# A two-layer graph kernel: neighbour lists for groups of 16 nodes instead of 32, sums on 32x32 tiles of TensorE, two blocks of nodes at a time

## The chip, the cores and the metric

One core of a Trainium2 chip runs the whole program. The metric is the device time of one execution in microseconds (us). Engines are named as in the profile: PE (TensorE matmul), PEld (its weight loads), DVE (VectorE), ACT (ScalarE), POOL (GpSimd), SP (SyncE, which here only issues DMAs).

## The reference

Two graph layers on N = 3327 nodes with D = 512 features. adj is sparse: the average row holds a few entries, but nodes with a low index have many (hubs).

```
# layer 0
h   = relu(layernorm(x));            x = x + adj @ (relu(adj @ (h @ W1) + b1) @ W2) + b2
# layer 1, on h = relu(layernorm(x))
sum_a  = adj @ h                                          # also adj @ (h @ W_gcnb)
attn_a = sigmoid([sum_a, h] @ Wa.T + ba);  attn_b = sigmoid([sum_a, h] @ Wb.T + bb)
hw     = h @ W_sa
e      = where(adj != 0, exp(-leaky_relu(hw @ a_left + (hw @ a_right).T)), 0)
x_a    = (e / (e.sum(1) + 1e-5)) @ hw;     x_b = adj @ (h @ W_gcnb) + b_gcnb
x      = x + sigmoid(attn_a * x_a + attn_b * x_b)
```

## The kernel before

N is padded to 3328: 26 blocks of 128 nodes (block 0 holds the hubs). The host hands over adj transposed, so that 128 rows of adjT are 128 source nodes (the contraction) and its columns are targets. All is float32.

**Stage A, first pass over adj (0 to about 232 us).** The columns of adjT are taken in seven chunks from the back, six of 512 and the last of 256. For each chunk 26 tiles of 128 rows are loaded on SP's queue (`load_adj`, a pool of eight buffers) and multiplied into `acc_u` (L568). DVE reduces each tile to the largest absolute value per group of 32 columns (`most`, L572). During the first chunk x is loaded and normalized as well and u = h @ W1 is made.
From `most` a generator, `make_lists`, makes the neighbour lists of a chunk while the next chunk is multiplied; one step of the generator is taken per tile. For each group of GW = 32 targets and each half (64 rows) of a block of lists, it holds which source nodes have an entry. It flags non-empty columns, scans them (L443 to L459), counts with two small matmuls (L465, L466) and one shifted matmul (L476), compares the place numbers with each row's offset (`at`, L502, on DVE), picks with small matmuls (`p_list`, L513), and turns the result into row numbers (L519 to L533): `row_h` for the rows of h, `row_a` for the pieces of adj. A list is padded to a fixed number of places: 64 places are one "room". `rooms` gives the rooms of each block, 0 for block 0 (done densely), then 8, 7, 6, 5, 5, six times 4, and 3 for the rest. If a list were longer, a dense fallback at the end of the program would run; with these inputs it does not.
As soon as lists are there, POOL gathers the 32-wide pieces of adj that they name (`gather`, L166, out is `ae`), one gather of 128 rows after another; `gather_behind` puts one behind three of four matmuls. At a chunk's end ACT makes gT (L343) and issues DMAs on its own queue: weights, the hub columns, the rows of g (`g_rows`), and for the ten blocks in OWN the block's own diagonal part (`load_own`), for which then no list entry is needed.

**Stage B, second pass (about 232 to 471 us).** The chunks 0 to 2303 are multiplied densely with g (`acc_g`, L825). For the last two chunks (blocks 18 to 25) the same product is made from the lists: 48 gathers of g rows and `acc_s` (L784), at the tiles named in SUMS. `make_h1` then makes x1 and h of layer 1 (`px` L663, layernorm, `score` L623, `own_logits` L630) and stores the rows of h in DRAM. `own_logits` is left for stage C in the blocks of LATE and OWN. Between tiles the hub block is done densely (`acc_hub`, L709).

**Stage C, attention (first gather of h at 455.6 us, to the end).** Blocks 25 down to 1, one at a time:
- `attend`: POOL gathers the h rows of the block's lists (128 rows of 2080 bytes each, out is `hr` or `rows`), DVE and ACT make the masked exponentials beside the adj pieces in `ae` (L950, L954, L249 to L251, L959). `fetch_ae` puts two gathers of adj (AE_PER) between, as long as there are any.
- `sums` (L981): for each list, adj and exponentials together (64 columns) times the gathered rows. A matmul uses a 64x64 tile of the array, that is, a quarter.
- `copy_out` (ACT, L1054, L1058), `turn` (transposes L995, DVE copy L1010), `weigh` (products `p_b` L1035 and `p_a` L1042), `finish`.
On PE the order is written out: weigh(block i+2), turn(block i+1), sums(block i). `pace` lets the first gather of a block wait for the sums of the block LEAD = 3 (in the last part of the blocks: 4) places earlier, so that POOL doesn't run into buffers in use. `issue_after` (here `queued`) keeps the written order on each engine.

```
columns = gather_adj()                     # a generator: one gather of adj at a time
NR, GR, AE_PER = 12, 24, 2
pairs = cycle(rows[1:3] + own + rows[3:] + rows[:1])   # 16 buffers of two rows per partition
```

Of the kernel before, what the change touches and what calls it, by code (L numbers as in the profile page):

```python
# [9 lines left out]
F32 = mybir.dt.float32  # L10
# [10 lines left out]
GW = 32  # L21
NQ = P // GW
HALF = P // 2
ROW = 520
LEAD = 3, 4
# [13 lines left out]
LATE = 10, 11, 16  # L39

OWN = 1, 6, 7, 8, 12, 13, 14, 15, 17, 18


def list_rooms(n_blocks):

    rooms = [0, 8, 7, 6, 5, 5] + 6 * [4]
    return (rooms + n_blocks * [3])[:n_blocks]
# [3 lines left out]
def kernel(  # L51
# [35 lines left out]
    rooms = list_rooms(NB)  # L87
    extra = [int(i in OWN) for i in range(NB)]
    first = [2 * sum(rooms[:i]) for i in range(NB)]
    NL = 2 * sum(rooms)  # L90


# [21 lines left out]
    for _ in range(WAKE):  # L114
# [21 lines left out]
    ae = [  # L136
        kept([P, 2 * (r + extra[i]), 2 * GW], f"ae{i}") if r else None for i, r in enumerate(rooms)
    ]

    def segments(i):  # L140

        r = rooms[i] + extra[i]
        n = -(-r // SEG)
        cuts = [-(-r * k // n) for k in range(n + 1)]
        return list(zip(cuts, cuts[1:]))
    hubp = ctx.enter_context(tc.tile_pool(name="hubp", bufs=6))
# [26 lines left out]
    listed, fetched = set(), [0] * NB  # L173

    def gather_adj():

        order = []
        for n, (c0, w) in enumerate(back):
            order += range(c0 // P, (c0 + w) // P)[:: 1 if n < LISTED else -1]
        for i in order:  # L180
            if not i:
                continue
            r = rooms[i]
            for k0, k1 in segments(i):
                for q in range(2):
                    for k in range(max(k0, extra[i]), k1):
                        while (i, q) not in listed:
                            yield None
                        f = first[i] + q * r + k - extra[i]
                        fetched[i] += 1  # L190
                        yield gather(
                            ae[i][:, 2 * k0 + q * (k1 - k0) + k - k0, :GW], adj_groups,
                            row_a[:, f : f + 1], NP * NG - 1,
                        )

    def load_own(i):

        n = segments(i)[0][1]
        for h in range(2):
            rows = slice(i * P + h * HALF, i * P + (h + 1) * HALF)  # L200
            nc.scalar.dma_start(
                ae[i][h * HALF : (h + 1) * HALF, 0 : n + 1 : n, :GW],
                adjT[rows, rows].rearrange("j (q i) -> j q i", i=GW),
            )
# [54 lines left out]
    with (  # L259
        tc.tile_pool(name="l0", bufs=1) as l0,  # L260
        tc.tile_pool(name="l0w", bufs=2) as l0w,
        tc.tile_pool(name="adjp", bufs=8) as adjp,
    ):

        def load_adj(j, c, name, n=1):

            c0, w = c
            t = adjp.tile([P, CW], F32, tag="adj", name=f"{name}_{c0}_{j}")
# [100 lines left out]
        lower = kept0([P, 1], "lower", F32)  # L369
        place_row = kept0([P, max(rooms) * HALF], "place_row", F16)  # L370
# [3 lines left out]
        def make_constants():  # L374
# [4 lines left out]
            for h in range(2):  # L379
                nc.vector.memset(apart[h * HALF : (h + 1) * HALF, 2 * h : 2 * h + 2], 0.0)  # L380
# [6 lines left out]
            for t, op, base in ((before, ALU.is_gt, 0), (shift, ALU.is_equal, -1)):  # L387
# [7 lines left out]
            nc.vector.memset(lower, 1.0)  # L395
            nc.gpsimd.affine_select(
                lower, lower, pattern=[[0, 1]], compare_op=ALU.is_ge, fill=0.0, base=-HALF,
                channel_multiplier=1,
            )
            first_iota = nc.gpsimd.iota(  # L400
                place_row, pattern=[[1, max(rooms) * HALF]], base=0, channel_multiplier=0,
# [9 lines left out]
            for r in sorted(set(rooms[1:])):  # L411
                i0, n = rooms.index(r), rooms.count(r)
                cols = slice(first[i0], first[i0] + n * 2 * r)
                nc.gpsimd.memset(limit[:, NQ * i0 : NQ * (i0 + n)], float(r * HALF))
# [907 lines left out]
```

## Time and profile before

| | |
|---|---|
| runs | 829.47, 836.75, 842.9 us; median 836.75 |
| the profiled execution | 834.5 us, span from first to last instruction 832.8 |
| busy: PE, DVE, POOL, ACT | 735.6, 506.0, 461.1, 194.5 us |
| granted TensorE clock, mean | 0.94 |
| gathers on POOL (L166) | 436: 194 of adj, 194 of h (120 to `hr`, 74 to `rows`), 48 of g |
| sums L981 | 480 + 296 + 80 matmuls |
| DMA | 185.08 MB, 222 GB/s over the span |

The profile comes from one execution and its page gives busy times by engine, the chain of work that ended last (each piece followed back to what released it), and groups of instructions by source line with busy time, mean duration in ns, and the idle time before them with its releaser. A window is a stretch of the span with the busy time of each engine in it. In POOL's timeline each line is one gather with the idle time before it in brackets.

### The profile page before, as it was taken

The numbers are of one execution on the slowest core, as the hardware profiler recorded it, in microseconds if no ns is written. First come the engines' busy times: TensorE is split into PE (matmuls) and PEld (weight loads), VectorE is DVE, ScalarE is ACT, GpSimd is POOL, SyncE is SP. The second block draws the span as 40 slices with busy tenths as digits, with TensorE's granted clock in tenths as the row PEclk, the third lists the DMA queues.
The fourth block names the chain that finished last, engine by engine and source line by source line (L and its number), as shares of the span: only waits on it lengthen the run. The fifth ranks groups of instructions, "written<-read, shape, count | busy, mean of one in ns | idle before, by whom it ended". The sixth has DMA issues, their size and how long they took to land.

```text
span 832.8 us, 11907 instructions
## 1 busy us (share of the span) xinstructions
PE 735.6 (88%) x3595; PEld 404.5 (49%) x3595; DVE 506.0 (61%) x1625; ACT 194.5 (23%) x402; POOL 461.1 (55%) x490
## 2 busy tenths in 40 slices
PE   9999888989899771999899749967999999999995
PEld 7774333444543220444355236633656655665554
DVE  7778868898860611798987225523665557553552
ACT  7770000000000110354544002211212222221121
POOL 2201756766657776534456766674657666767500
PEclk9999989999999875999999969996999999999999
DMA  8788988988878844789994755664667877767510
GB/s 271 245 287 259 326 246 242 293 272 246 232 232 284 262 132 134 240 279 312 327 314 135 241 150 145 199 185 115 195 211 244 255 206 233 240 205 234 178 51 29
DMA packets 104889, 185.08 MB, mean 222 GB/s; under 512 B 18401, under 2 KB 35441, under 8 KB 104818
## 3 DMA queue, kind: packets, MB, share of 16 engines
q1 hardware_dynamic: 66544, 113.43, 41.8%
q0 software_dynamic: 23264, 57.64, 24.3%
q10 hardware_dynamic: 15010, 13.18, 4.9%
q8 instruction: 30, 0.49, 0.2%
q14 instruction: 41, 0.34, 0.1%
HBM read 162.29 MB, written 22.26 MB: 222 GB/s over the span
## 4 chain that ended last, share of the span: by engine, by line
PE 72%; DVE 7%; issue 6%; another core or an unknown queue 6%; DMA 5%; ACT 2%; POOL 1%; SPq 1%; DVEq 0%; ACTq 0%; POOLq 0%
PE acc_u L568 17%; PE acc L981 12%; PE p_b L1035 11%; PE p_a L1042 10%; PE acc_g L825 8%; PE pu L333 3%; PE ptt L995 3%; DMA a<-in_adjT_dram 2%; PE acc_hub L709 2%; PE px L663 2%; PE pt L325 1%; DMA xb<-in_x_dram 1%; PE acc_s L784 1%; DMA hr<-h_rows,row_h 1%
## 5 line engine op out<-in xcount | busy, mean ns | idle before, releaser
L166 POOL DMA_INDIRECT ae<-in_adjT_dram,row_a x194 | 202.6, 1044 | 181.8 <-DVE past L519 54.3
L568 PE MATMUL acc_u<-a,rows 128*128 128x512 f32 (+1 forms) x364 | 161.0, 583 | 0.5 <-DMA a<-in_adjT_dram 0.5
L166 POOL DMA_INDIRECT hr<-h_rows,row_h x120 | 122.7, 1022 | 62.5 <-issue 27.4
L825 PE MATMUL acc_g<-a,g 128*128 128x512 f32 (+1 forms) x260 | 117.1, 584 | 7.2 <-DMA a<-in_adjT_dram 6.8
L572 DVE TENSOR_REDUCE most<-a 128x16 f32<-128x512 f32 (+1 forms) x182 | 112.3, 638 | 11.6 <-issue 6.3
L1035 PE MATMUL p_b<-W_g_sb,tyT 128*128 128x257 f32 x416 | 99.3, 391 | 15.8 <-DVE tyT L1010 15.3
L1035 PEld LDWEIGHTS p_b<-W_g_sb,tyT 128*128 128x128 f32 x416 | 77.8, 192 | 46.5 <-DVE tyT L1010 15.6
L166 POOL DMA_INDIRECT rows<-h_rows,row_h x74 | 75.1, 1015 | 44.3 <-PE acc L981 20.9
L568 PEld LDWEIGHTS acc_u<-a,rows 128*128 128x128 f32 x364 | 67.2, 195 | 58.8 <-issue 56.0
L1042 PE MATMUL p_a<-W_sa_sb,tyT 128*128 128x512 f32 (+2 forms) x216 | 94.2, 577 | 0.2
L1010 DVE COPY tyT<-ptt 128x512 f32<-128x512 f32 x51 | 34.8, 685 | 87.0 <-PE p_a L1042 31.7
L825 PEld LDWEIGHTS acc_g<-a,g 128*128 128x128 f32 x260 | 50.0, 200 | 58.5 <-issue 44.9
L981 PE MATMUL acc<-hr,ae 64*64 64x512 f32 x480 | 68.3, 614 | 4.4 <-issue 4.0
L166 POOL DMA_INDIRECT g_row<-g_rows,row_h x48 | 49.0, 1021 | 20.9 <-issue 13.4
L1042 PEld LDWEIGHTS p_a<-W_sa_sb,tyT 128*128 128x128 f32 x216 | 40.7, 189 | 38.8 <-issue 36.9
L884 ACT ACTIVATE f<-f 128x2 f32<-128x2 f32 x26 | 5.3, 203 | 192.4 <-DVE f L883 97.2
L981 PEld LDWEIGHTS acc<-hr,ae 64*64 64x64 f32 x480 | 27.6, 136 | 33.6 <-issue 33.0
L343 ACT ACTIVATE gT<-acc_u,b_col 128x512 f32<-128x512 f32 (+1 forms) x7 | 4.6, 656 | 163.8 <-DMA a<-in_adjT_dram 90.9
L663 PE MATMUL px<-W_sb,sT 128*128 128x512 f32 x52 | 26.7, 650 | 15.4 <-ACT sT L799 12.0
L666 DVE TENSOR_TENSOR xb<-px,xb 128x512 f32<-128x512 f32 x26 | 17.3, 682 | 36.6 <-PE px L663 28.5
L981 PE MATMUL acc<-rows,ae 64*64 64x512 f32 x296 | 37.1, 593 | 2.5 <-issue 2.3
L623 DVE SCALAR_TENSOR_TENSOR junk<-rows,w_rows 128x512 bf16<-128x512 f32 x52 | 35.6, 684 | 3.2 <-ACT rows L244 1.1
(159 smaller groups left out, 945.2 us busy)
## 6 DMA issues: line engine op xcount, KB each, us to landing
a<-in_adjT_dram SPq DMA_DIRECT2D x286, 256.0 KB
h_rows<-rows SPq DMA_DIRECT2D x26, 260.0 KB
x<-in_x_dram SPq DMA_DIRECT2D x26, 256.0 KB
xb<-in_x_dram SPq DMA_DIRECT2D x26, 256.0 KB
x<-xb ACTq DMA_DIRECT2D x26, 256.0 KB
x1b<-x SPq DMA_DIRECT2D x26, 256.0 KB
out_dram<-va SPq DMA_DIRECT2D x25, 256.0 KB
ae<-in_adjT_dram,row_a POOLq DMA_INDIRECT x194
```

What stands on the lines that cost most here:

```text
L166: return nc.gpsimd.indirect_dma_start(out=dst, out_offset=None, in_=table, in_offset=bass.IndirectOffsetOnAxis(ap=rows, axis=0), bounds_ch ...
L333: nc.tensor.matmul(pu[:, :HID], hT[:, k, :], W1_sb[:, k, :], start=(k == 0), stop=(k == KD - 1))
L568: added = nc.tensor.matmul(acc[:, :w], u[j], a[:, :w], start=(j == 0), stop=(j == NB - 1))
L572: nc.vector.tensor_reduce(most[:, : w // GW, j], a[:, :w].rearrange("p (b i) -> p b i", i=GW), axis=AX.X, op=ALU.max, apply_absolute_value ...
L623: return nc.vector.scalar_tensor_tensor(junk, h, 1.0, w_rows[:, s, :], op0=ALU.mult, op1=ALU.mult, accum_out=into)
L663: last_row[2] = nc.tensor.matmul(px, sT[:, b * P : (b + 1) * P], W2_sb, start=True, stop=True)
L825: added = nc.tensor.matmul(acc[:, :w], g[j], a[:, n % per, :], start=(n == 0), stop=(n == NB - 1))
L981: added = nc.tensor.matmul(taken[i]["acc"][h][q * HALF : (q + 1) * HALF, :], both[half_p, q * n + k, :], taken[i][k0][k][half_p, q, :D], s ...
L995: moved = nc.tensor.transpose(pt[:, k * P : (k + 1) * P], ty[h][:, k * P : (k + 1) * P], ident)
L1010: last = nc.vector.tensor_copy(dst, src)
L1035: nc.tensor.matmul(p_b[n][:, :WH], tyT[:, k, 0, :], W_g_sb[:, k, n * WH : (n + 1) * WH], start=(k == 0), stop=(k == KD - 1),)
L1042: last = nc.tensor.matmul(p_a[:, c0:c1], tyT[:, k, 1, :], W_sa_sb[:, k, c0:c1], start=(k == 0), stop=(k == KD - 1),)
```

## The change

- Lists are made for groups of 16 targets (GW = 16). Blocks are handled in teams: block 1 alone, and twelve pairs (2,3) to (24,25). A pair's 128 partitions are cut into four quarters: two blocks by two halves; a room is then 32 places for each of them. Rooms per team are 5, 7, 5, 5, 4, 4, 4, 4, 3, 3, 3, 3, 3, with four lists (q) each: 53 x 4 = 212 gathers of adj and as many of h. All pairs load their own diagonal parts, by eight DMAs per pair, and their own h rows.
- `sums` works on 32x32 tiles: four quarters (r) by four lists (q), each 512 columns.
- In stage C the order is one team at a time: weigh and turn for the two blocks of the team before (`weigh_all`, with a `turn` between `p_b` and `p_a` of the last), then the team's sums. LEAD is 2 teams; `fetch_ae` takes four gathers per team. Block 0 is copied and turned before the first sums.
- The comparisons `at` are made by ACT as a steep sigmoid (STEEP = 200) instead of by DVE.
- adj is loaded in pieces of two tiles (512 KB), five buffers; `most` is reduced over two tiles at once.
- LATE grows from three to nine blocks; no block's `own_logits` is skipped in stage B on account of OWN. The list sums of stage B use a copy of the adj pieces that ACT places in a 32-wide tile (`diag`), and start at other tiles (SUMS).

```diff
-GW = 32
+GW = 16
-LEAD = 3, 4
+LEAD = 2
-LATE = 10, 11, 16
-OWN = 1, 6, 7, 8, 12, 13, 14, 15, 17, 18
-    rooms = [0, 8, 7, 6, 5, 5] + 6 * [4]
-    return (rooms + n_blocks * [3])[:n_blocks]
+LATE = 8, 10, 11, 12, 13, 14, 15, 16, 17
+def make_teams(n_blocks):
+    teams = [(1,)] + [(i, i + 1) for i in range(2, n_blocks, 2)]
+    rooms = [5, 7, 5, 5, 4, 4, 4, 4] + n_blocks * [3]
+    return teams, rooms[: len(teams)]
...
+    def tiles_of(m):
+        return [
+            (slice(r * tall[m], (r + 1) * tall[m]), teams[m][r // 2], r % 2)
+            for r in range(P // tall[m])
+        ]
...
+    def load_own(m):
+        n = segments(m)[0][1]
+        for part, i, h in tiles_of(m):
+            for s in range(2):
+                nodes = own_rows(i, h, s)
+                nc.scalar.dma_start(
+                    ae[m][part, 2 * s * n : (2 * s + 1) * n + 1 : n, :GW],
+                    adjT[nodes, nodes].rearrange("j (q i) -> j q i", i=GW),
+                )
...
-        tc.tile_pool(name="adjp", bufs=8) as adjp,
+        tc.tile_pool(name="adjp", bufs=5) as adjp,
...
-            t = adjp.tile([P, CW], F32, tag="adj", name=f"{name}_{c0}_{j}")
+            t = adjp.tile([P, 2 * CW], F32, tag="adj", name=f"{name}_{c0}_{j}")
...
-                        nc.vector.tensor_scalar(
-                            at[:, k : k + r, h, :],
-                            place_row[:, : r * HALF].rearrange("p (k m) -> p k m", m=HALF),
-                            offset[:, b : b + 1], None, op0=ALU.is_ge,
-                        )
+                        nc.scalar.activation(
+                            at[:, k : k + r, part],
+                            place_row[:, : r * t].rearrange("p (k m) -> p k m", m=t),
+                            AF.Sigmoid, bias=offset[:, b : b + 1], scale=STEEP,
+                        )
...
-                with queued(scaled[min(j + 3, NB - 1)] if n == 0 else None):
-                    nc.vector.tensor_reduce(
-                        most[:, : w // GW, j], a[:, :w].rearrange("p (b i) -> p b i", i=GW),
+                both = 2 if n else 1
+                if j % both == 0:
+                    tiles = tile_a[:, j % per : j % per + both, :]
...
-        SUMS = {1: (14, 16, 18, 20, 24), 2: (16, 18, 20, 22, 25)}
+        SUMS = {1: (2, 15, 19, 24), 2: (3, 17, 21, 25)}
...
             for k in range(n):
-                for q in range(2):
-                    for h in range(2):
-                        half_p = slice(h * HALF, (h + 1) * HALF)
+                for q in range(4):
+                    for r, (part, i, h) in enumerate(tiles_of(m)):
                         added = nc.tensor.matmul(
-                            taken[i]["acc"][h][q * HALF : (q + 1) * HALF, :],
-                            both[half_p, q * n + k, :], taken[i][k0][k][half_p, q, :D],
+                            taken[m]["acc"][r][q * QW : (q + 1) * QW, :],
+                            both[part, q * n + k, :], taken[m][k0][k][q][part, :D],
...
+        for m in range(M - 1, 0, -1):
+            with queued(*held):
+                for seg in segments(m):
+                    made = attend(m, seg)
...
+            fetch_ae(2 * AE_PER)
+            held, turned = [], []
+            added = weigh_all(added)
+            with queued(added):
+                for seg in segments(m):
+                    added = sums(m, seg)
```

## The prediction

> **What bounds the kernel now.** I read the page first: busy times, then the chain that ended last, then the costliest groups; after that the windows by stage, and at last POOL's own timeline. The page:
>
> ```profile
> PE 735.6 (88%) x3595; PEld 404.5 (49%) x3595; DVE 506.0 (61%) x1625; ACT 194.5 (23%) x402; POOL 461.1 (55%) x490
> PE 72%; DVE 7%; issue 6%; another core or an unknown queue 6%; DMA 5%; ACT 2%; POOL 1%; SPq 1%; DVEq 0%; ACTq 0%; POOLq 0%
> L166 POOL DMA_INDIRECT ae<-in_adjT_dram,row_a x194 | 202.6, 1044 | 181.8 <-DVE past L519 54.3
> L166 POOL DMA_INDIRECT hr<-h_rows,row_h x120 | 122.7, 1022 | 62.5 <-issue 27.4
> L981 PE MATMUL acc<-hr,ae 64*64 64x512 f32 x480 | 68.3, 614 | 4.4 <-issue 4.0
> ```
>
> PE is the bound by share, and the listed sums (L981) are 12% of the chain. POOL looks free at 55%. The windows (stage A: first pass over adj with the lists; B: second pass; C: attention) correct that; the columns are the stretch, its length, then PE, PEld, DVE, ACT and POOL busy, granted clock, DMA share, GB/s:
>
> ```profile
> 0.00:232.00 232.00, 212.82 (x1104) 121.25 (x1104) 189.29 (x532) 51.20 (x113) 113.03 (x153) 0.96 0.85 263
> 320.00:440.00 120.00, 102.52 (x358) 48.84 (x357) 92.61 (x308) 50.63 (x85) 57.50 (x54) 0.93 0.85 279
> 560.00:786.00 226.00, 217.44 (x1210) 126.88 (x1209) 118.63 (x428) 49.52 (x109) 146.84 (x144) 0.96 0.70 212
> 786.00:833.00 47.00, 37.52 (x228) 23.29 (x226) 21.84 (x78) 9.38 (x22) 0.00 (x0) 0.95 0.13 42
> ```
>
> A lives on DMA (0.85), PE and DVE close together; C is PE's, and POOL has nothing after 786. But POOL's busy time leaves out what it does between gathers. Its timeline (start, length, idle before in brackets), and two pieces of the chain in time:
>
> ```profile
> 577.46 0.99 POOL L166 DMA_INDIRECT rows<-h_rows,row_h  x1 [7.54 <-PE acc L981]
> 578.76 1.00 POOL L166 DMA_INDIRECT rows<-h_rows,row_h  x1 [0.31 <-issue]
> 580.07 1.00 POOL L166 DMA_INDIRECT rows<-h_rows,row_h  x1 [0.30 <-issue]
> ...
> 585.28 1.00 POOL L166 DMA_INDIRECT ae<-in_adjT_dram,row_a  x1 [0.30 <-issue]
> 586.58 0.99 POOL L166 DMA_INDIRECT ae<-in_adjT_dram,row_a  x1 [0.31 <-issue]
> ```
> ```profile
> 473.05 16.46 another core or an unknown queue
> ...
> 585.37 3.49 PE acc L981 x30
> 588.86 3.67 PE p_b L1035 x16
> 592.53 3.43 PE p_a L1042 x8
> ```
>
> Back to back a gather takes one step of 1.303 us, whether its rows are of adj or of h. Stage C runs 217 of them (194 of h, 23 of adj) from 455.6 to 785.3: 217 x 1.303 = 283 of 330 us. So POOL has 47 us of idle time in C, nearly all of it the wait for the sums of an earlier block (`pace`, releaser PE L981 above). That is the cover this change uses.
>
> **The change part by part.** The sum is made against the profiled execution: 834.5 us, span 832.8 (1.7 around it). The median of the runs is 836.75, 1.0027 times that.
>
> *Sums on 32x32 tiles.* Before: 856 instructions (480+296+80); a block of 32 takes 3.49 us, 0.109 us each, so 93 us of PE. A full-array 512-column instruction takes 3.43/8 = 0.43 us (p_a), so four tiles side by side lose nothing. After: 12 pairs x 2 x 16 tiles x (48+12 rooms)/12 = 1920, plus 80 for block 1: 2000. Sixteen side by side: 0.43/16 = 0.027 us, 54 us, saves 39. No row shows 16 tiles. The nearest from the other side is the list sums (L784, 64x32, 128 columns): 24 in some 0.82 us, 0.034 each, whatever the width: 68 us, saves 25. Only if tiles of this size did not overlap further would it be 0.109: 218 us, loses 125. I take 68, the row nearest in shape.
>
> [...]
>
> What PE needs in C is then 26 x (10.8 - 2.63 of sums) = 212 us for turns and products (10.8 us is the step from p_b to p_b of a three-room block) plus 68: 280 us, against 305 before.
>
> *Gathers.* Rooms: 53 x 4 = 212 lists of adj and 212 of h, against 194 each: +36, 47 us of POOL. The built order of POOL's queue says where: before the first h gather 169 adj gathers stand (171 before), so C gets 43 of them (23 before). C on POOL: (212+43) x 1.303 = 332.3 us, +49.5. By team: a three-room pair asks 16 gathers, 20.8 us, of POOL and 2 x 8.17 + 32x4x0.034 = 20.7 of PE: even. Four rooms: 26 to 21.8; five: 31 to 23. So POOL sets C, and the 25 us that PE saves turn into waits of PE for gathered rows. Halving the row of an adj gather (128 to 64 bytes) doesn't help: the step is the same for 2080-byte rows.
>
> How much of the 47 idle us stays? LEAD is now two pairs, four blocks, about as far ahead as before, and PE is faster, so pacing waits shrink: 5 us (start-up only) to 47 (as now). I take 18, because PE is as slow as POOL in the five three-room pairs, and because of the stall of 16.46 us above: PE, ACT and DVE stood during a run of 24 gathers without a gap (455.6 to 486.7) and went on some 3 us after POOL paused. Pieces of the same name stand in B at 265 (9.13), 308 (8.78) and 318 (13.65). The cause isn't in the trace; but C will now be one long run of gathers. The tail after the last gather was 47.5 us, with PE two blocks behind; the least is the last sums to the end, 810.1 to 832.8, plus one attend, 28. I take 38.
>
> *Lists in A.* p_list goes from 388 to 808 matmuls; a group of 12 takes 0.29 to 0.36 us between acc_u steps, so 420 x 0.027 = 11 us more of PE, which the DMA share of 0.85 hides in part; bare it is 11. DVE loses about 100 comparisons (0.22 us from start to start, 22 us); it gains twice the width in flag, scan, after and step (0.46+1.01+0.58+0.58 = 2.6 a chunk, 16 in all); the reduction over two tiles saves the fixed part of one per pair (L572: 676 ns at 512 columns, 408 at 256, so 140 ns fixed; 13 a chunk, 11 us in six). About 17 us of 189 less. ACT gains 200 sigmoids (the 192-wide activation took 0.369, the 128-wide 0.305: 61 to 74 us), one table load of 1.28, and 76 more own-part DMA issues at some 0.65 us (49 us), plus 16 for g_own. ACT is busy 51 of 232 us, so it fits; but within a chunk eight issues per pair stand ahead of the sigmoids, so the lists come late: in the built order most p_list groups stand after tiles 12 to 26 of the 26, where before they stood after tiles 8 to 14. Behind a p_list that waits on ACT stand acc_u, then gT, and the next chunk. Cost: from -10 (DVE relieved, DMA free) to 6 chunks x 6 us = +36. I take +5.
>
> [...]
>
> *adj in pieces of two tiles.* 143 loads for 286, ten tiles in flight for eight. SP's queue issues half as many; the bytes and the DMA share stay. acc_g's wait for adj is 6.8 us in all, so at most 7 gained, and at the start of a chunk a piece of 512 KB lands later than one of 256. Taken at 0, between -7 and +4.
>
> *B.* Nine blocks are LATE and no OWN block is skipped, so 17 instead of 13 own_logits run in B, at 1.7 us of DVE: +7 in a stretch where DVE is busy 93 of 120. List sums get 16 copies on ACT (0.37 each, 6 us, ACT 51 of 120: at nothing; 6 bare). I take +5 for B (0 to 13). The nine late ones (15 us of DVE, 5 before) lie under the first gathers of C, 12 us to the first rows' landing; 0 taken, 10 at most.
>
> *Sum.* First h gather 455.6 + 5 (A) + 5 (B) + 332.3 (gathers) + 18 (pauses) + 38 (tail) = 853.9; + 1.7 = 855.6; x 1.0027 = **858 us**.
>
> **The rivals.**
> *Faster: the stalls go.* Against 858: B's three pieces (9.13+8.78+13.65 = 31.6 us) vanish, and pauses fall from 18 to 4: 858 - 46 = 812. For it: list sums and their gathers start earlier in B and are spread, DVE does less in A, and pieces of adj are larger. Against: 217 gathers precede C, as many as before less two. It decides from 38 us on, the distance from 858 to 820.
> *No change: the idle time takes it all.* +49.5 of gathers into 47 us of idle, A and B at nothing, tail as before: 834.5 + 2.5 = 837, x 1.0027 = 839. For it: POOL's waits in C are nearly all `pace`. Against: a queue without slack passes on every hiccup.
> *Late lists.* PE waits 6 us for ACT's sigmoids in each of six chunks: 858 + 31 = 889.
> *Sixteen tiles are no faster than four:* 839 + 125 = 964. Against: 64x32 tiles already go at 0.034.
>
> **How the numbers follow.** Forecast 0.40; faster 0.32; no change 0.21; late lists 0.05; no overlap 0.02. The three runs before spread by 13 us, 1.6%, so 2% is about what a measurement can tell. Slower: 0.40+0.05+0.02 = 0.47. The range goes from 803 (the faster rival with DMA's -10 in A) to 890 (late lists); the forecast alone, by pauses 5 to 47 with tails 28 to 47 not both at their ends, is 832 to 885.
>
> **What would show it.** Right: in C, POOL's gathers at 1.303 us with idle under 25 us in all, PE idle before L-sums on hr or rows by a DMA releaser; a pair's 32-tile sums at 0.03 to 0.04 us each; gT times later by a few us each chunk. Wrong: POOL paused by PE as often as now (then PE, not POOL, bounds C); sums at 0.1 us; B 30 us shorter or a first h gather well ahead of 455.

## The result and the profile after

The changed kernel takes **1024.52 us** (median of 4 runs, 1013.93 to 1029.38) beside 839.83 us of the kernel before on the same chip (4 runs, 829.47 to 843.69). The ratio is 1.2255, with a 95% interval of 1.204 to 1.2471: 22 to 23% slower. This ratio, like all that follow, is that of the means of the runs within 1.5% of each kernel's fastest, the others (the profiled one here, by a hair) counting as slow. The profiled execution took 1029.38 us, with a span of 1027.6. The forecast was 858, in a range of 803 to 890. The sign was right, the size was not.

The page of the changed kernel, the lines that answer to those shown of before (L178 is `gather`, L1054 is `sums`):

```profile
PE 835.4 (81%) x5221; PEld 417.7 (41%) x5221; DVE 494.6 (48%) x1463; ACT 263.6 (26%) x625; POOL 499.8 (49%) x510
PE 48%; DVE 12%; another core or an unknown queue 12%; DMA 11%; issue 10%; ACT 4%; POOL 2%; ACTq 1%; SPq 0%; POOLq 0%; DVEq 0%
L178 POOL DMA_INDIRECT hr<-h_rows,row_h x140 | 141.2, 1008 | 126.1 <-PE acc L1054 73.9
L178 POOL DMA_INDIRECT rows<-h_rows,row_h x72 | 73.4, 1019 | 72.5 <-PE acc L1054 50.0
L1054 PE MATMUL acc<-hr,ae 32*32 32x512 f32 (+1 forms) x1040 | 108.5, 810 | 9.5 <-issue 8.8
L1054 PE MATMUL acc<-h_own,ae 32*32 32x512 f32 x384 | 40.9, 882 | 85.5 <-DVE tyT L1083 66.3
```

Before, the gathers of h into `rows` stood as

```profile
L166 POOL DMA_INDIRECT rows<-h_rows,row_h x74 | 75.1, 1015 | 44.3 <-PE acc L981 20.9
```

Two readings decide. POOL waits for PE's sums before its gathers of h, more than before (73.9 and 50.0 us, lines 3 and 4), which the forecast named as a sign of being wrong; and PE now waits 66.3 us for DVE before its sums (last line of the page's), for a copy `tyT` of 0.7 us. PE's share of the chain fell from 72% to 48%, and "another core or an unknown queue" doubled to 12%. The windows by stage (length; PE, PEld, DVE, ACT, POOL busy; granted clock, DMA share, GB/s): the first pass A from 65, stage B, C from the first to the last gather of h, and the tail:

```profile
65.00:278.00 213.00, 174.24 (x1101) 73.82 (x1100) 138.36 (x238) 65.99 (x208) 107.42 (x100) 0.89 0.73 216
278.00:506.90 228.90, 186.85 (x759) 85.92 (x760) 136.42 (x463) 78.36 (x157) 125.93 (x117) 0.89 0.71 223
506.90:967.40 460.50, 361.64 (x2658) 179.10 (x2658) 148.84 (x524) 61.23 (x129) 258.07 (x255) 0.83 0.59 164
967.40:1027.60 60.20, 49.24 (x316) 29.80 (x315) 21.15 (x69) 11.56 (x26) 0.00 (x0) 0.94 0.14 45
```

Against the same points of before (last gT 231.6, first gather of h 455.6, last one's end 785.3, end 832.8) A (last gT at 277.9) lost 46.3 us, B 5.0, C 130.8 and the tail 12.7: together 194.8, the difference of the spans. In C the clock is 0.83 and the DMA share 0.59, PE is busy 361.64 and POOL 258.07 of 460.50 us: nothing is full. The chain shows what happens in one team (start, length, what):

```profile
695.69 10.84 another core or an unknown queue
...
707.58 4.62 another core or an unknown queue
...
712.97 8.70 PE acc L1054 x152
```

And three engines in the same stretch, first POOL (in brackets the idle time before, and its releaser), then DVE, then PE:

```profile
683.63 1.00 POOL L178 DMA_INDIRECT hr<-h_rows,row_h  x1 [10.63 <-PE acc L1054]
...
708.75 1.00 POOL L178 DMA_INDIRECT ae<-in_adjT_dram,row_a  x1 [0.31 <-issue]
722.04 1.00 POOL L178 DMA_INDIRECT rows<-h_rows,row_h  x1 [12.29 <-PE acc L1054]
```
```profile
694.94 0.75 DVE L966 SCALAR_TENSOR_TENSOR vb<-vb,r,va 128x512 f32<-128x512 f32 x1 [0.81 <-issue]
706.55 0.43 DVE L961 TENSOR_TENSOR vb<-p_b,bg_row 128x257 f32<-128x257 f32 x1 [10.87 <-remote]
```
```profile
691.42 3.63 PE L1108 MATMUL p_b<-W_g_sb,tyT 128*128 128x257 f32 x16
...
699.50 1.05 PE L1054 MATMUL acc<-h_own,ae 32*32 32x512 f32 x4
712.97 1.75 PE L1054 MATMUL acc<-h_own,ae 32*32 32x512 f32 x14 [12.42 <-DVE tyT L1083]
```

POOL runs 20 gathers without a break, 683.63 to 709.75. PE's records of the `p_b` that DVE waits for end at 695.05; DVE goes on only at 706.55, and for the next piece at 712.22, 2.5 us after POOL has stopped. PE waits for that copy and goes on with its sums at 712.97, after a first four. POOL's next run waits (`pace`) for these sums and starts at 722.04. So POOL and PE take turns: run of gathers, then sums, then the next run. It looks like the 16.46 us stall of before, now in most teams. I call it the hold-up: while POOL's gathers run on without a break, PE's completions (or its work) come some 8 to 17 us late.

The trace of before holds a second one in C, which the prediction does not name. POOL ran 24 gathers from 538.89 to 569.92; the block's `p_b` came 30.9 us after the one before instead of 10.8 to 11.7, and DVE stood:

```profile
572.87 0.43 DVE L891 TENSOR_TENSOR vb<-p_b,bg_row 128x257 f32<-128x257 f32 x1 [13.76 <-remote]
```

The three pieces in B (265, 308, 318 us) lie in or just behind runs of 24 (240.10 to 271.72) and 20 (302.42 to 328.14) as well.

### The profile page after: what moved, and what is told of

Its sections match the earlier page's. It is cut to its first block, busy times and chain, and to the rows that moved or that the text cites. A ratio compares the mean times of both kernels' runs of the same rounds, so it can differ in the third digit from the quotient of the medians.

```text
span 1027.6 us, 15177 instructions
## 1 busy us (share of the span) xinstructions
PE 835.4 (81%) x5221; PEld 417.7 (41%) x5221; DVE 494.6 (48%) x1463; ACT 263.6 (26%) x625; POOL 499.8 (49%) x510
## 2 busy tenths in 40 slices
DMA packets 113127, 192.96 MB, mean 188 GB/s; under 512 B 23197, under 2 KB 40721, under 8 KB 113042
## 4 chain that ended last, share of the span: by engine, by line
PE 48%; DVE 12%; another core or an unknown queue 12%; DMA 11%; issue 10%; ACT 4%; POOL 2%; ACTq 1%; SPq 0%; POOLq 0%; DVEq 0%
PE acc L1054 16%; PE acc_u L607 6%; PE acc_g L895 6%; PE p_b L1108 5%; PE p_a L1116 4%; DMA a<-in_adjT_dram 4%; PE pu L348 2%; DMA xb<-in_x_dram 2%; DVE most L614 2%; DMA ae<-in_adjT_dram 2%; PE acc_hub L767 2%; POOL hr L178 1%; DVE tyT L1083 1%; ACT at L531 1%
## 5 line engine op out<-in xcount | busy, mean ns | idle before, releaser
L178 POOL DMA_INDIRECT ae<-in_adjT_dram,row_a x212 | 227.1, 1071 | 221.1 <-PE acc_u L607 90.6
L178 POOL DMA_INDIRECT hr<-h_rows,row_h x140 | 141.2, 1008 | 126.1 <-PE acc L1054 73.9
L607 PE MATMUL acc_u<-a,rows 128*128 128x512 f32 (+1 forms) x364 | 177.2, 610 | 6.3 <-issue 4.5
L614 DVE TENSOR_REDUCE most<-a 128x64 f32<-128x1024 f32 (+1 forms) x104 | 104.1, 1012 | 54.2 <-DMA a<-in_adjT_dram 42.8
L1054 PE MATMUL acc<-hr,ae 32*32 32x512 f32 (+1 forms) x1040 | 108.5, 810 | 9.5 <-issue 8.8
L1054 PE MATMUL acc<-h_own,ae 32*32 32x512 f32 x384 | 40.9, 882 | 85.5 <-DVE tyT L1083 66.3
L178 POOL DMA_INDIRECT rows<-h_rows,row_h x72 | 73.4, 1019 | 72.5 <-PE acc L1054 50.0
L531 ACT ACTIVATE at<-place_row,offset 128x96 bf16<-128x96 f16 (+4 forms) x200 | 61.1, 393 | 108.7 <-DMA a<-in_adjT_dram 57.2
L1054 PE MATMUL acc<-rows,ae 32*32 32x512 f32 x576 | 64.8, 808 | 3.7 <-issue 3.3
L178 POOL DMA_INDIRECT g_row<-g_rows,row_h x48 | 49.8, 1037 | 31.8 <-ACT at L531 14.8
L1054 PEld LDWEIGHTS acc<-hr,ae 32*32 32x32 f32 (+1 forms) x1040 | 33.2, 121 | 69.9 <-issue 66.3
L961 DVE TENSOR_TENSOR vb<-p_b,bg_row 128x257 f32<-128x257 f32 x26 | 11.1, 426 | 84.9 <-remote 62.1
L1054 PEld LDWEIGHTS acc<-h_own,ae 32*32 32x32 f32 x384 | 6.9, 122 | 102.4 <-DVE tyT L1083 80.2
```

The source lines that it names most:

```text
L178: return nc.gpsimd.indirect_dma_start(out=dst, out_offset=None, in_=table, in_offset=bass.IndirectOffsetOnAxis(ap=rows, axis=0), bounds_ch ...
L531: nc.scalar.activation(at[:, k : k + r, part], place_row[:, : r * t].rearrange("p (k m) -> p k m", m=t), AF.Sigmoid, bias=offset[:, b : b ...
L607: added = nc.tensor.matmul(acc[:, :w], u[j], a[:, :w], start=(j == 0), stop=(j == NB - 1))
L614: nc.vector.tensor_reduce(most[:, : w // GW, j : j + both], tiles.rearrange("p k (b i) -> p b k i", i=GW), axis=AX.X, op=ALU.max, apply_ab ...
L961: read_b = nc.vector.tensor_tensor(vb[:, :WH], p_b[0][:, :WH], bg_row[:, :WH], ALU.add)
L1054: added = nc.tensor.matmul(taken[m]["acc"][r][q * QW : (q + 1) * QW, :], both[part, q * n + k, :], taken[m][k0][k][q][part, :D], start=(k0 ...
```

## The experiments

The first theory: a long unbroken run of gathers holds PE up, whatever the bytes, and `pace` then makes POOL wait in turn. Its rivals: the bytes do it; POOL's rate alone does it; the 32x32 sums themselves are dear; and for A, the lists, the pieces of adj, or ACT.

The kernels ran in several groups. In a group all ran on one chip, beside the kernel before. There were two kinds of chip: on one kind the kernel before takes 829 to 842 us (medians), on the other 734 to 739. On the second kind the hold-up didn't appear. "Kind of chip" is a reading: each chip was used once, and the groups on the first kind all ran before those on the second, so a state that changed with time isn't told apart from the chip. Each number stands beside its own before.

### Runs of 8 to 12 in place of 16 to 20 (e1_spread)

```diff
+                        if k0 + k == extra[m] + 2 and not q and len(combined) >= LEAD:
+                            pace(gathered[0], marks[-1])
...
+            marks.append(last)        # the last p_b of the team's second block
```


> The changed kernel, with one more pace in each team: the gathers of the third room and what follows wait for the p_b of the second block of the team before, so that POOL's 16 to 20 gathers come in runs of about 8 and 8 to 12 with a pause between. Theory A (in a run of more than some nine gathers without a pause the completions of PE reach the other engines late, until the run ends; then POOL's run and PE's sums follow each other instead of overlapping): the step of a three-room pair falls from 31 us to 24 to 26, of a four-room pair from 38 to 27 to 31; whole time 920 to 960. Rival B (the rate of the gathers, 1.30 us each, bounds stage C): an added wait can only cost, 1020 or more. Rival C (the sums on 32x32 tiles are what is slow): no change, 1015 to 1030.

Measured: 1002.13 us (998.2 to 1006.06) beside 842.42; ratio 1.1894 [1.1716, 1.2073]. A three-room team went from 31 us to 28.4. The gain (a ratio of 1.1894 in place of 1.2255, the intervals just touching) is a fraction of what was expected. The reason stands in PE's timeline: POOL's second run (651.0 to 666.3, twelve gathers) now falls on the sums, and these come a few at a time until it ends:

```profile
661.09 3.33 PE L1056 MATMUL acc<-hr,ae 32*32 32x512 f32 x5 [0.80 <-issue]
664.64 1.86 PE L1056 MATMUL acc<-hr,ae 32*32 32x512 f32 x3 [0.22 <-issue]
```

Eight sums took 5.4 us here; at the 0.034 us a record measured in e2 below they take 0.3. PE's idle time is put down to "issue": it waits for nothing that the trace shows. Runs of eight didn't help the sums either: the three-room team at 626.68 has POOL in a run of eight (622.59 to 632.73), and its 128 records take 12.2 us, where e2's take 4.3.

### The h rows by plain DMAs (e2_no_h_gather)

```diff
-                        with queued(gathered[0]):
-                            gathered[0] = gather(
-                                hr[k][q], h_dram[:, :], row_h[:, f : f + 1], NP - 1
-                            )
-                        if k0 + k + q == extra[m] and len(combined) >= LEAD:
-                            pace(gathered[0], combined[-LEAD])
+                        nc.sync.dma_start(
+                            hr[k][q], h_dram[f % NB * P : (f % NB + 1) * P, :]
+                        )
```


> The changed kernel, but the 212 gathers of h rows in stage C are plain DMAs on SP's queue of as many bytes (whole blocks of h instead of the listed rows, so the sums are over other rows). POOL keeps only the gathers of adj. Theory A: no long run of gathers is left in C, so PE goes at its own pace, 24 us per pair, C about 330 us instead of 520; whole time 820 to 870. Rival D (the bytes or packets of the gathered rows, not POOL's runs, hold PE's completions back): the stalls stay, over 980. Rival C: sums as long as before this edit, C not under 450, over 950.

Measured: 906.81 us beside 842.42. The total was missed, because C started later (first `p_b` at 589.7 instead of 555.9); why wasn't looked into. C itself fell from 472 us (first `p_b` to the end) to 315, a three-room team from 31 to 20.8, a four-room team from 38 to 21.8, the same bytes still flowing (192.95 MB in all, 192.96 before the edit), and no hold-up is left. That speaks against the bytes as its cause, and it shows what the sums cost without it. A window over one team's sums, of the changed kernel and then of this one:

```profile
674.80:683.25 8.45, 8.45 (x125) 3.35 (x125) 5.06 (x24) 1.52 (x3) 0.00 (x0) 0.58 0.07 19
```
```profile
642.50:646.80 4.30, 4.30 (x128) 2.12 (x113) 2.46 (x9) 1.52 (x3) 0.00 (x0) 1.00 0.13 37
```

4.30/128 = 0.034 us a record at a granted clock of 1.00, as forecast; 8.45/125 = 0.068 at 0.58, after PE has stood for 10.79 us:

```profile
674.80 2.58 PE L1054 MATMUL acc<-h_own,ae 32*32 32x512 f32 x15 [10.79 <-DVE tyT L1083]
```

So the hold-up is paid twice, as a wait and as a slow clock after it.

### Comparisons back on DVE (e3_at_dve)

```diff
-                        nc.scalar.activation(
...
-                            AF.Sigmoid, bias=offset[:, b : b + 1], scale=STEEP,
+                        nc.vector.tensor_scalar(
...
+                            offset[:, b : b + 1], None, op0=ALU.is_ge,
```


> The changed kernel with the comparisons back on DVE (200 of them, is_ge). If the lists of stage A are late because ACT issues own-part DMAs (16 in 13.6 us) before it compares, stage A ends 25 to 40 us earlier (at 240 to 255 instead of 278) and the whole time is 985 to 1000. If DVE, with 200 comparisons of 0.2 us more, is the tighter engine, stage A ends no earlier and the time is 1020 or more.

Measured: 998.95 us beside 842.42. A ends at 242.9 instead of 277.9, the first gather of h stands at 476.3 instead of 506.9. So 35 of the 46 us that A lost hang on where the comparisons wait.

### The kernel before with runs of 16 (e4_before_long)

```diff
-                    lead = LEAD[i < NB - 8]
-                    if k0 + k + q == extra[i] and len(combined) >= lead:
+                    lead = 2
+                    if i % 2 == 0 and k0 + k + q == extra[i] and len(combined) >= lead:
```


> The kernel before, with pace only at every second block and two blocks ahead instead of at each block and three or four ahead: POOL's gathers in stage C come in runs of 16 or more instead of 8; nothing else. Theory A: PE's completions come late in each run and each pair of blocks loses 4 to 9 us: 880 to 950. Rival B (rate) and any theory that puts the loss on the new lists or tiles: within 12 us of before, 830 to 850.

Measured: 929.72 us beside 842.42; ratio 1.1035 [1.0899, 1.1171]. The sums, lists and loads are those of before; the edit is in which blocks wait, and for which sums. The run of 16 from 534.73 to 555.3 holds up PE's products, which need no gathered row (chain, in time):

```profile
550.21 1.75 issue
551.96 0.38 PE p_b L1035
552.34 1.79 issue
```

So the hold-up does not need the 32x32 sums.

### The kernel before with some of its long runs cut (e5_before_short)

```diff
-LEAD = 3, 4
+LEAD = 3, 3
...
-        gather_g(GR)
+        gather_g(GR // 3)
...
+                if c == 0 and n in (14, 24):
+                    gather_g(GR // 3, added)
...
+                    if NB - 4 < i < NB - 1 and k0 + k + q == extra[i]:
+                        pace(gathered[0], attended[-1])
```


> The kernel before with its three long runs of gathers cut: the 24 gathers of g rows at the start of stage B go 8 by 8 behind acc_g, the gathers of blocks 24 and 23 wait each for the exponentials of the block before, and LEAD is 3 throughout (the change from 3 to 4 let 24 gathers run on at 539 us). Theory A: the pieces of 9.1 us at 265, 16.5 at 473 and some 24 between 549 and 573 shrink; 795 to 825. Rival B (rate of the gathers): added waits cost, 840 or more.

Measured: 831.78 us (10 runs) beside 828.94; ratio 0.998 [0.992, 1.004], no gain. The stall at 549 was gone (`p_b` of that block 550 to 564.7, before 546 to 577), but one stayed (`p_b` from 478.3 to 502.6). It is no counterexample: the edit left a run of 24 there, from 474.74 to 505.74, and DVE stands inside it. The late blocks, with the smaller lead, gave the rest back (steps of 15 to 17 us instead of 12.5).

```profile
501.60 0.37 DVE L967 TENSOR_REDUCE es<-ae 128x64 f32<-128x192 f32 x1 [9.17 <-remote]
```

### Gathers paced in fours (e6_runs_of_4)

The comparisons are on DVE as in e3, and every fourth gather is to wait for a mark on PE.

```diff
+                        if len(marks) >= 4:
+                            pace(g, marks[-1])
...
+                        room = k0 + k - extra[m]
+                        if 0 < room < 4 and not q and len(combined) >= LEAD and len(marks) >= 4:
+                            pace(gathered[0], marks[(-3, -2, -1)[room - 1]])
```


> The changed kernel with the comparisons on DVE as in e3_at_dve, and stage C's gathers paced in fours: each room and the adj gathers wait for another product of the team before. Theory A: three-room pairs step by 24 to 26 us instead of 31, PE's clock stays whole; 890 to 950. If short pauses don't help, as much as e3_at_dve with the gain of e1_spread: 970.

Measured: 985.19 us beside 828.94, a miss: by its own before no better than e3 (1.188 and 1.186 times). The sums still come a few at a time after their first 38 records or so. But POOL's runs weren't of four. The later marks had mostly been passed when POOL came to them, and a team's gathers went as four, a pause, and then 12 or 16 without one; POOL's waits about a three-room team, the third opening the next team:

```profile
584.03 0.99 POOL L178 DMA_INDIRECT hr<-h_rows,row_h  x1 [7.30 <-PE acc L1059]
...
590.99 1.00 POOL L178 DMA_INDIRECT rows<-h_rows,row_h  x1 [2.06 <-PE p_b L1097]
...
614.34 1.00 POOL L178 DMA_INDIRECT rows<-h_rows,row_h  x1 [7.63 <-PE acc L1059]
```

So this run says nothing of runs of four. That the length of the run isn't all, e1 shows: runs of eight, harmless in the kernel before, held up the 128 small records there (12.2 us instead of 4.3), while products and turns got through. This suggests that the number of PE's instructions counts as well; it isn't shown.

### The pieces of adj alone (e7_before_adj2)

```diff
-        tc.tile_pool(name="adjp", bufs=8) as adjp,
+        tc.tile_pool(name="adjp", bufs=4) as adjp,
...
-            t = adjp.tile([P, CW], F32, tag="adj", name=f"{name}_{c0}_{j}")
+            t = adjp.tile([P, 2 * CW], F32, tag="adj", name=f"{name}_{c0}_{j}")
```


> The kernel before with adj in pieces of two tiles, four buffers (eight tiles as before), and the reduction over two tiles at once; nothing else of the change. If the larger pieces are what costs in stage A (3 to 11 us that e3_at_dve left over there): 845 to 860. If not: 830 to 845.

Measured: 834.52 us (8 runs) beside 828.94; ratio 1.0082 [1.0032, 1.0132]; A ends at 230.0. The larger pieces aren't what A lost.

### POOL busy with something else (e8_rest)

```diff
+            run[0] += 1
+            if run[0] % 8 == 0:
+                for _ in range(4):
+                    with queued(gathered[0]):
+                        gathered[0] = nc.gpsimd.memset(idle, 0.0)
```


> The changed kernel with four memsets on POOL (2.4 us in all) after each eighth gather of stage C: POOL stays busy, but no run of gathers is longer than eight. Theory A in the form that the gathers' own queue has to drain: the dribble goes, three-room pairs step by 25 to 28 us instead of 31, 940 to 980. In the form that any work of POOL keeps PE waiting: no gain, 1015 to 1060.

Measured: 985.39 us beside 828.94. Adding about 2.4 us of work to POOL after every eighth gather made the kernel faster (three-room teams 27 to 28 us instead of 31). It is the gathers that hold PE up, not that POOL is busy. In C POOL hardly waits any more (one rest, and the window of C):

```profile
597.09 2.50 POOL L989 MEMSET idle<- 128x576 f32 x4
...
506.93:932.95 426.02, 385.42 (x2751) 182.84 (x2749) 150.87 (x528) 64.77 (x139) 330.57 (x379) 0.91 0.65 178
```

255 gathers at 1.303 and 31 rests (379 - 255 = 124 memsets) at 2.4 are 332 + 74 = 406 of these 426 us, which leaves some 20 of waits, where the changed kernel had 128. PE's sums still come a few at a time, but POOL no longer waits for them: what the rests saved in waits they cost for the greater part in POOL's own time.

### More PE instructions in the kernel before (e9_before_split2, e12_before_split4), its shorter runs again (e11_before_short2), half the sums (e10_half_the_sums)

e9 and e12 cut the 512 columns of a sum into two or four instructions. e11 is e5 with fewer waits in the late blocks, and e10 is e6 with every second room of sums left out.

```diff
+                        wide = D // 2 if k0 + k else D          # e12: D // 4
+                        for f0 in range(0, D, wide):
+                            cols = slice(f0, f0 + wide)
...
```
```diff
-                    lead = LEAD[i < NB - 8]
+                    lead = 2 if i == NB - 5 else LEAD[i < 9]
...
+                    if NB - 5 < i < NB - 1 and k0 + k + q == extra[i]:
+                        pace(gathered[0], attended[-1])
```
```diff
+            taking = range(0, rooms[m] + extra[m], 2)
...
-                for q in range(4):
+                for q in range(4 if k0 + k in taking else 0):
```


> The kernel before, with each 512-column matmul of the listed sums (all but a block's first room) cut into two of 256 columns: 1512 matmul records in the sums instead of 856, about the same work of the array, the same gathers in the same runs of eight. Theory A2 (while POOL issues gathers, only a few PE instructions per us get through, from a reserve of a hundred or two; so what counts is PE instructions per gather, not the length of a run alone): blocks step by 11 to 13 us instead of 10.8; 845 to 890. Theory A in its first form (runs of eight are safe): 825 to 842.

> The same with four matmuls of 128 columns: 2824 records in the sums, more than the 2000 of the changed kernel. By 0.034 us per record of this width PE needs 0.4 us more per block, 10 us in all. Theory A2: blocks step by 13 to 16 us; 890 to 980. First form of theory A: 835 to 855.

> A second try at a version better than both: the kernel before with the cuts of e5_before_short, blocks 24 to 22 waiting each for the exponentials of the block before, and LEAD 4 only from block 8 on, where a block has ten and more gathers. Theory A: the stalls at 473 and 549 go and the late blocks don't lose what e5_before_short lost there; 800 to 820. If what is cut comes back elsewhere: 825 to 835.

> e6_runs_of_4 (the changed kernel, comparisons on DVE, gathers of stage C paced in fours), leaving out every second room of the listed sums: some 64 matmul records per three-room pair instead of 128, all gathers, exponentials and products kept. PE saves 2.2 us per pair by itself, 26 to 30 us in all. Theory A2: the dribble inside the sums goes too, three-room pairs step by 21 to 24 us instead of 30; 985 falls to 880 to 925. Rival E (it isn't PE's instructions but the gathers that set the step): 950 to 965.

Measured, beside 733.83 us: 737.01 (8 runs, ratio 1.0054 [1.0009, 1.0099]); 833.18 (1.136 [1.1285, 1.1436]); 742.8 (1.013 [1.0066, 1.0195]); 809.46. This chip was of the kind without the hold-up, so none of the four answers the question it was made for. e12's loss is of another sort, with no hold-up in its trace: a quarter piece takes 0.075 us (5.23 us for 70 records), and a block 13.4 us instead of 10.9 in e9; why four pieces are dear and two are not wasn't asked. e10 ran 245 gathers without a break (425.3 to 748.7) with no hold-up. That led to the next two.

### Changed kernel and e4 again, on a chip without the hold-up (f1_after_again, f2_before_long_again)

No edit; f2 is e4's kernel.

> The changed kernel as it is, beside the kernel before. Theory F (the hold-up depends on the chip; without it POOL's gathers bound stage C, 255 x 1.303 = 332 us without a pause): where before takes some 734 us, this takes 780 to 820; where before takes 830 to 842, this takes 1010 to 1030. If the hold-up belongs to the change whatever the chip: over 900 in both.

> The kernel before with long runs (as e4_before_long). Theory F: 730 to 745 where before takes 734, 920 to 935 where before takes 830 to 842. If long runs cost anywhere: 10% above before in both.

Measured, beside 734.89 us: f1 840.11 (840.0 to 840.21; ratio 1.1425 [1.1379, 1.147]), f2 740.56. Runs of 16 in the kernel before cost 87 us on the first kind of chip and 6 here. f1's own expectation (780 to 820) was missed by 20 us. Here f2 is within 1% of before and serves as its trace. The windows A, B, C and tail of f1, and then of f2:

```profile
65.00:260.50 195.50, 169.65 (x1100) 72.60 (x1098) 137.98 (x237) 65.10 (x208) 107.09 (x100) 0.90 0.81 235
260.50:446.80 186.30, 172.34 (x760) 81.06 (x761) 136.67 (x465) 78.12 (x158) 127.94 (x118) 0.97 0.87 274
446.80:794.90 348.10, 288.15 (x2784) 179.56 (x2783) 151.56 (x537) 64.34 (x137) 258.61 (x255) 0.91 0.78 218
794.90:838.50 43.60, 32.85 (x189) 20.32 (x187) 16.14 (x55) 7.73 (x18) 0.01 (x1) 0.86 0.20 61
```
```profile
65.00:215.20 150.20, 142.50 (x712) 67.15 (x711) 140.48 (x373) 4.12 (x6) 100.16 (x99) 1.00 0.95 294
215.20:399.00 183.80, 174.82 (x665) 82.72 (x664) 136.32 (x447) 67.56 (x122) 133.06 (x122) 0.98 0.89 293
399.00:706.50 307.50, 298.92 (x1693) 177.65 (x1695) 169.32 (x595) 68.82 (x153) 223.05 (x215) 0.99 0.75 221
706.50:738.80 32.30, 23.09 (x142) 15.00 (x134) 13.57 (x51) 6.64 (x16) 0.99 (x1) 0.94 0.18 56
```

The differences are 45.3 us in A, 2.5 in B, 40.6 in C and 11.3 in the tail, together 99.7. C in f1 is the picture of the forecast: 255 gathers in 348.1 us are 332 of gathering and 16 besides, most of it one wait after 237 gathers without a pause, while PE is busy 288.15 us, eleven less than in f2's shorter C.

```profile
774.17 1.00 POOL L178 DMA_INDIRECT hr<-h_rows,row_h  x1 [11.43 <-PE acc L1054]
```

### The own parts' DMAs issued by SP (f4_own_on_sp)

```diff
-                nc.scalar.dma_start(
+                nc.sync.dma_start(
...
+                if n and j in (6, 14):
+                    for m in teams_in(*back[n - 1])[j // 14 :: 2]:
+                        load_own(m)
```


> The changed kernel with its 96 own-part loads issued by SP, eight at a time in the next chunk's sixth and fourteenth tile; the comparisons stay on ACT. If ACT's DMA issues are what delays the lists: stage A ends at 235 to 250 instead of 278 (on a chip where before takes 830) or at 225 to 240 instead of 260 (where it takes 734), the time falls by 15 to 35. If the comparisons themselves are too slow on ACT, or SP's own queue suffers as much: within 8 us of the changed kernel's stage A.

Measured: 817.62 us beside 738.66. A ends at 232.7, where f1's ended at 260.5. That names the cause of the greater part of A's loss: not the sigmoids themselves, which are still on ACT here, but the DMA issues ahead of them. ACT in the changed kernel (ACTq is its issuing of DMAs), and then PE's longest waits for the lists there ("issue": no releaser seen) and in f1; in f4 the waits for L531 are 1.9 us:

```profile
107.98 13.55 ACTq L216 DMA_DIRECT2D ae<-in_adjT_dram  x16
121.64 8.59 ACT L531 ACTIVATE at<-place_row,offset 128x96 bf16<-128x96 f16 x32 [26.62 <-issue]
```
```profile
PE p_list L542 <- issue: 25.6, 14, 4.5
```
```profile
PE p_list L542 <- ACT at L531: 18.8, 5, 4.5
```

Sixteen issues take 13.55 us, 0.85 each, and the chunk's sigmoids stand behind them. The total fell by 22.5 us against f1, which ran on another chip of the kind.

### No gathers of adj in C (f5_no_adj_in_c)

```diff
-                with queued(gathered[0]):
-                    gathered[0] = next(columns, None) or gathered[0]
+                pass
...
-            while fetched[m] < 4 * r:
-                fetch_ae(1)
```


> The changed kernel without the 43 gathers of adj that stand in stage C (their lists weigh nothing: the teams concerned sum less, with as many instructions). Where before takes 734 us: if POOL's rate bounds C, 43 x 1.303 = 56 us less, 780 to 795 instead of 840; if PE bounds it, 825 to 840. Where before takes 830 to 842: runs of 12 to 16 gathers instead of 16 to 20, each step 5 us shorter: 960 to 985 instead of 1024.

Measured: 809.8 us beside 738.66. C with the tail took 367.5 us, f1's 391.7: 24 less for 43 gathers, worth 56 at 1.303. That lies between what was expected if POOL bounds C (780 to 795) and if PE does (825 to 840). POOL then needs 276 of the 322.6 us between its first and its last gather of h, and waits 43.6 for PE's sums. POOL's rate is the bound in C by a narrow margin only.

## Why the prediction was wrong, step by step

**A, priced at +5, measured +46.3: wrong on both kinds of chip (45.3 on the second).** The text saw that eight issues per pair stand ahead of the sigmoids and that p_list, acc_u and gT wait behind. The failed step is the choice between -10 and +36, made in favour of "it fits, ACT is busy 51 of 232 us". A share says nothing of an order: 0.85 us an issue instead of the 0.65 taken, 16 of them at a stretch, made the lists late. Even +36, the upper end given for A, was 10 too low. The trace of before had the dearer issue as well as the cheap one (0.65 and 0.94 us each):

```profile
124.91 1.30 ACTq L201 DMA_DIRECT2D ae<-in_adjT_dram  x2
...
129.50 3.76 ACTq L201 DMA_DIRECT2D ae<-in_adjT_dram  x4
```

f4 takes 27.8 us of it away by moving the issues (against f1), e3 35.0 by moving the comparisons (against the changed kernel); each pair is from two chips of one kind. The rival "late lists" named the mechanism; its six waits of 6 us, 36 in all, were near. What is left with f4 (17.5 us against f2) wasn't split further; the added p_list matmuls, estimated at 11, may be part of it.

**Pauses in C, priced at 18, measured 460.5 - 332.3 = 128: the term that failed most.** The text described the 16.46 us stall, tied it to a run of 24 gathers, wrote that "C will now be one long run of gathers", and then charged part of 18 us for it. The step that failed is to price a stall as a single event when its trigger becomes the normal state. The profile of before had both stalls of C in its two runs of 24, and in its runs of 6 to 10 no wait of DVE with an unknown releaser above 3.4 us; and the change made runs of 16 and 20 the rule. Measured, POOL waits 18 times for PE's sums in C, 123.9 us (73.9 + 50.0), up to 12.3 at a time; a three-room team takes 31 us where its gathers need 20.8, a four-room team 38 for 26. e4 shows it on the kernel before (+87 us), e2 shows C without it (315 instead of 472), f1 shows the same kernel with 16 us of pauses on a chip without it. With that the term's 18 fits the chip without the hold-up, not the one that it was meant for.

**The tail, priced at 38 where before had 47.5, measured 60.2.** The forecast let it shrink; it grew by 12.7, and on the second kind of chip, by f1 and f2, by 11.3 (32.3 to 43.6). That 43.6 lies in the 28 to 47 given is chance, since before is shorter there. What the forecast left out is the order on PE, one team of two blocks at a time. From the first sums of the last team (988.77) to the end it takes 38.8 us, in f1 41.6, with four groups of products (991.50 to 1005.98) between these sums and the team's second ones; the 28 was built on the 22.7 us from the last sums of before to the end. On the first kind there is a backlog besides: PE reaches those sums 21.4 us after POOL's last gather here, and 2.0 us after it in f1.

**Right.** B: 5 forecast, 5.0 measured (2.5 on the second kind); its parts weren't measured one by one. Sums on 32x32 tiles: 0.034 us a record, 12.6 times as fast as the 0.43 of a full-array one, at the granted clock of 1.00 that e2 has there. The row that gave the 0.034 was of other tiles and 128 columns, so that it held for 512 was a good guess. POOL as the bound of C at 1.303 us a gather: f1's 237 gathers without a pause show it where the hold-up is absent; f5 limits this, since only 24 of 56 us came back. That gathers, pauses and tail were forecast at 332.3 + 18 + 38 = 388 and f1 has 391.7 is luck, for there they follow on 339.8 of f2, and here they were to follow on 377.2. Pieces of adj at nothing in A: e7 has A at 230.0 for 231.6.

The sum with the measured terms (the pauses being what is left of C): 455.6 + 46.3 + 5.0 + 332.3 + 128.2 + 60.2 = 1027.6, the span. The range's lower end was mis-summed: 812 with A at -10 in place of +5 is 797, not 803. The rivals fell: the stalls did not go (812), and idle time didn't absorb the gathers (839). That f1's 840 lies near the forecast says little, since the kernel before takes 735 there.

**The clock after a wait.** The trace has 0.58 over 8.45 us of sums after 10.8 us of waiting, 0.66 over 6.84 us after 5.4 in another team, and 1.00 in e2 where PE didn't stop. Within the first of these stretches the clock stayed low for long: 0.50 from 674.80 to 681.00, 0.79 from there to 683.25. The 125 records took 8.45 and 6.84 us, where e2's 128 took 4.30. How long a wait brings the clock down, and how long it takes to come back, these windows alone don't tell.

**Left open.** What joins POOL's gathers and PE's progress, and why one kind of chip shows it and the other doesn't, isn't settled. e2 and e8 leave the gathers themselves; e1 beside the kernel before suggests that the number of PE's instructions counts too, and the runs made to test that (e9, e12, e10) fell on chips without the hold-up. All executions were recorded by the profiler, so none tells whether recording takes part.

No variant beat the kernel before on either kind of chip; of the changed kernel with its whole computation, f4 came nearest, 817.62 beside 738.66.

## What to carry to other kernels

When a profile shows a stall whose cause you can't name, note what else runs at that moment, and count how often the change will bring that state about; then price the stall that many times, not once. ACT, free by its share (112.41 us busy of the changed kernel's first 278), still delayed the sigmoids that stood behind 13.55 us of DMA issues in its queue, so place issues by order and not by busy time. A change that moves load to the engine with slack should be costed per step (here 20.8 us of gathers to 20.7 of PE): where both sides come out even, a hiccup of one can be passed to the other (460.5 us of C for 332.3 of gathers).

## What the hardware did that was not expected

- On one kind of chip, runs of 16 to 24 back-to-back gathers held PE up by some 8 to 17 us (DVE's longest wait in each of 7 teams 8.0 to 12.4, in the two stalls of before 13.8 and 16.5); the last of what was held came 1 to 3 us after the run ended (in C, 7 teams and both stalls of before). On the other, 237 gathers in a row (450 to 763 in f1) did nothing of the kind. The same changed kernel took 1024.5 us on the first and 840.1 on the second; the kernel before took 839.8 and 734.9.
- After such a wait PE's granted clock was 0.66 and 0.58 in two teams, and the sums took 0.055 and 0.068 us a record, against 0.034 at 1.00 in e2.
- Adding 2.4 us of other work to POOL after every eighth gather, on the first kind, made the program faster than without it (985.39, one execution, beside a before of 828.94; 1024.52 beside 839.83 for the changed kernel as it was).
